# Edge-by-row matrices of a four-layer graph network: made once and loaded by every layer, with the steps of one tile spread over more rounds

## The chip, the cores and the metric

The kernel runs on one core of a Trainium2 chip. Its engines are PE (matrix products), DVE (vector), ACT (scalar, activation functions), POOL (GpSimd) and SP, which here only starts DMAs. Each engine runs its own instructions in order; an instruction waits for what it needs through semaphores. The metric is the device time of one execution in microseconds, the median of several runs.

## The reference

Four graph layers over 4096 nodes of 256 features each work on the same adjacency matrix `adj` (4096 x 4096, about nine neighbours a node beside the node itself). Each layer normalizes the rows of x, takes the positive part, computes attention scores for every pair of nodes, masks them with `adj`, takes a softmax over the neighbours, and adds the weighted sum to x:

```
for layer in (0, 1, 2, 3):
    h = maximum(layernorm(x), 0)
    x = x + gnn[layer](h, adj, ...)
```

Layer 0 has eight heads, with a bias from curvature features. Layer 1 has one head with leaky-ReLU scores from two vectors. Layer 2 takes two softmaxes, of e and of -e, and multiplies both results with a matrix `wtrans`. Layer 3 has four heads whose scores are products of the rows themselves; entries that are not neighbours count there as score 1.

## The kernel before

The kernel does not form the dense attention matrix. `gnn_lists` finds the edges and works on lists: the 4096 rows are 32 tiles of 128, and each tile has up to 9 x 128 = 1152 places for edges (EC = 9 chunks of 128). For each tile there is a matrix of zeros and ones that says which edge belongs to which row. It is needed in two orientations: rows on the partitions, edges along the free axis (`st`, 128 x 1152), and edges on the partitions, rows along the free axis (`s`, nine chunks of 128 x 128).

**Layer 0** runs together with the reading of the adjacency matrix. `piece` (L1094) loads 512 KB of it and turns it into a mask, `pack` (L1112) packs masks into keys by products, `rank` (L1134) sorts out the keys of a tile, `columns` (L1219) and `places` (L1255) decode them for four tiles at a time, `mark` (L1294) makes `st` of a tile and stores it to `rows_of` in DRAM, and `find_edges` (L1303) puts the column number of each edge on the partition of the edge by products with `st`, and writes it to `nbr`. Then come the steps of a tile: `begin0` (L1328) starts the gather of the neighbours' rows, `before0` (L1335) brings the row's own scores to its edges (L1343) and transposes the nine chunks of `st` on PE (L1355), which ACT copies into `s_f` (L1356); `score0`, `turn_d`, `curve` and `weigh0` compute the weights and multiply the gathered rows with them (L1388); `attend0` (L1390) sums over the edges by products with `s_f` (L891); `finish0`, `turn1` and `rows1` normalize the new rows and store the table of layer 1. All these are put on a plan with a due time each (from L1421 on), and are issued in the order of these times: PE works in exactly this order, and the order on the other engines is settled when the program is built.

**Gathers.** `gather` (L879) starts nine indirect DMAs on POOL (L881) for a tile, one a chunk, each of 128 rows of the table, and one DMA on SP (L885) for the tile's own rows. A layer's gathers need the whole table that the layer before has written. G0 = 5 and G1 = 6 are the numbers of buffers for gathered rows.

**Layers 1 to 3** are each a call of `run` (L1493), which issues rounds. In round r each step works on tile r minus the step's lag, so a step of lag 1 works on the tile before the one of lag 0. `loads` (lag -3) loads `st` and x of a tile through SP; `begin` (lag 2 - G1 = -4) starts the gather. `before12` (L1516) brings the row's scores to the edges and calls `s_chunks` (L1486), nine transposes into a PSUM tile `s_ps`. `weigh1` (L1540) and `weigh2` (L1607) compute the weights w and multiply `s_ps` with them into `sw` on DVE (L1545, L1620). `attend1` and `attend2` sum over the edges by products with `sw` (L891, L1636). `finish1`, `turn2`, `rows2`, and in layer 2 `signed2`, `turn_signed`, `through_wt`, `finish2`, `turn3`, `rows3`, complete the tile and store the table of the next layer. In layer 3 `before3` (L1719) casts `st` and the transposed chunks to float on ACT, and `weigh3`, `attend3`, `finish3` follow. The lags of layers 1 and 2 are in these lines (L1584 and L1704):

```
(0, weigh1), (1, finish1), (0, attend1), (1, turn2), (-1, before12(own[0])), (1, rows2),
(0, weigh2), (1, signed2), (2, finish2), (0, attend2), (2, turn3), (1, turn_signed),
(2, rows3), (-1, before12(own[1])), (1, through_wt),
```

In layers 0 and 3 the product of the gathered rows with the weights takes the weights from PSUM: ACT writes them there first (L1385, L1751).

## Time and profile before

| | us |
|---|---|
| median of 14 runs | 1741.99 |
| lowest and highest of them | 1736.57, 1747.43 |
| the profiled execution | 1739.59 |
| its span | 1737.9 |

Busy time over the span: PE 1339.5 us, DVE 1050.6, ACT 584.2, POOL 1113.8. The first gather starts at 132.5 us. The gathers of layer 0 are started from then to 533 us, those of layer 1 from 569 to 929, of layer 2 from 951 to 1313, of layer 3 from 1344 to 1705; the span ends 33 us later. HBM is read at 289.60 MB and written at 43.29 MB.

In the lines of a profile, L881 is line 881 of the kernel; `out<-in` names the tiles; `x32` is the number of instructions; "busy, mean ns" is followed by the idle time of the engine just before them and what ended it. "SPq" and "ACTq" are DMA starts on these engines' queues. PE's clock is given as the share of full speed that it was granted.

### The profile page before, as it was taken

The page shows a single profiled execution, that of the slowest core. Times are in us where ns is not written, and L with a number is a line of the kernel's source. Part 1 is how long each engine was busy: PE and PEld are TensorE (multiplying, and loading weights), DVE is VectorE, ACT ScalarE, POOL GpSimd, SP SyncE. Part 2 cuts the span into 40 slices and gives each one's busy share as a digit, 9 for nine tenths or more (in the row PEclk, how much of TensorE's full clock was granted, in tenths as well). Part 3 has the DMA queues.
Part 4 walks back from the last instruction along what each step waited for, and adds up shares of the span by engine and source line. Part 5 has one row for each costly group of instructions (what it writes and reads, how often), then busy time and mean ns, then how long its engine had stood idle before and what let it go on. Part 6 is the DMA issues. An engine that isn't in the chain of part 4 may idle for free.

```text
span 1737.9 us, 26840 instructions
## 1 busy us (share of the span) xinstructions
PE 1339.5 (77%) x8560; PEld 1072.3 (62%) x8560; DVE 1050.6 (60%) x3038; ACT 584.2 (34%) x1586; POOL 1113.8 (64%) x1208
## 2 busy tenths in 40 slices
PE   3765888878897477666675689988897798898984
PEld 2443666656776365555564577777775577776773
DVE  4675898888874233333332355555554688888884
ACT  2675666763432011111111133333343222222220
POOL 2007775755771677777773777777772777777771
PEclk9996898988998678878887799999998899999998
DMA  8988999984662666767664566666653555555541
GB/s 278 304 274 301 307 351 340 332 299 125 189 174 70 192 172 180 182 182 178 179 171 129 147 169 178 182 179 181 171 173 92 151 170 156 169 169 165 168 134 45
DMA packets 178342, 334.81 MB, mean 193 GB/s; under 512 B 36624, under 2 KB 108560, under 8 KB 178192
## 3 DMA queue, kind: packets, MB, share of 16 engines
q0 software_dynamic: 55296, 153.72, 33.3%
q1 hardware_dynamic: 73730, 133.50, 23.5%
q10 hardware_dynamic: 49166, 45.79, 7.7%
q8 instruction: 70, 1.15, 0.3%
q14 instruction: 80, 0.66, 0.1%
HBM read 289.60 MB, written 43.29 MB: 192 GB/s over the span
## 4 chain that ended last, share of the span: by engine, by line
PE 34%; POOL 16%; DVE 16%; DMA 13%; issue 10%; ACT 3%; DVEq 0%; ACTq 0%; POOLq 0%; SPq 0%
PE o L891 21%; POOL g L881 16%; DMA g<-table,nbr 11%; PE o L1636 3%; PE pt L851 2%; DVE sw L1545 2%; PE pv L1737 2%; DVE s L1742 2%; DVE sw L1620 2%; DVE v L1741 1%; DVE r L824 1%; PE kps L1120 1%; DVE stats L821 1%; PE pb L1343 1%; PE pt L842 1%
## 5 line engine op out<-in xcount | busy, mean ns | idle before, releaser
L881 POOL DMA_INDIRECT g<-table,nbr x1152 | 1097.9, 953 | 484.6 <-issue 311.1
L891 PE MATMUL o<-g,sw 128*128 128x257 f32 x640 | 214.0, 509 | 117.9 <-DVE sw L1548 117.9
L891 PE MATMUL o<-g,s_f 128*128 128x264 f32 (+1 forms) x1152 | 283.7, 403 | 0.0
L891 PEld LDWEIGHTS o<-g,sw 128*128 128x128 f32 x640 | 165.6, 264 | 156.4 <-DVE sw L1548 121.0
L891 PEld LDWEIGHTS o<-g,s_f 128*128 128x128 f32 x1152 | 234.2, 203 | 44.4
L1636 PE MATMUL o<-g,sw 128*128 128x257 f32 x768 | 185.5, 400 | 59.2 <-DVE sw L1620 59.2
L1636 PEld LDWEIGHTS o<-g,sw 128*128 128x128 f32 x768 | 150.2, 199 | 94.0 <-DVE sw L1620 71.3
L1737 PE MATMUL pv<-g,st_f 128*128 128x256 f32 x576 | 146.1, 400 | 45.9 <-DVE v L1741 45.9
L844 ACT COPY hT<-pt 128x256 f32<-128x256 f32 x128 | 47.3, 369 | 329.0 <-PE pt L842 321.3
L1737 PEld LDWEIGHTS pv<-g,st_f 128*128 128x128 f32 x576 | 107.7, 196 | 72.4 <-DVE v L1741 59.6
L1559 DVE RECIPROCAL inv<-o 128x1 f32<-128x1 f32 x32 | 5.4, 168 | 217.0 <-PE o L891 217.0
L1101 ACT ACTIVATE mask<-adj,minus_half 128x1024 bf16<-128x1024 int32 x112 | 124.8, 1142 | 31.1 <-DVE same L929 15.4
L1741 DVE TENSOR_TENSOR v<-pv,g 128x512 f32<-128x512 f32 (+1 forms) x160 | 96.1, 633 | 47.8 <-DMA g<-table,nbr 41.5
L851 PE MATMUL pt<-wcat,hT 128*128 128x272 f32 (+2 forms) x384 | 92.1, 357 | 25.2 <-ACT hT L844 25.1
L851 PEld LDWEIGHTS pt<-wcat,hT 128*128 128x128 f32 x384 | 64.8, 196 | 47.9 <-ACT hT L844 40.4
L1754 DVE TENSOR_TENSOR g<-g,pm 128x2560 f32<-128x2560 f32 x32 | 90.1, 2817 | 3.9 <-ACT pm L1751 3.8
L1388 DVE TENSOR_TENSOR g<-g,pb 128x2560 f32<-128x2560 f32 x32 | 90.1, 2815 | 1.2 <-ACT pb L1385 1.2
L1120 PE MATMUL kps<-mask,enc 128*128 128x512 bf16 x256 | 80.8, 416 | 3.9 <-ACT mask L1101 3.5
L1742 DVE TENSOR_REDUCE s<-v 128x36 f32<-128x2304 f32 x32 | 81.5, 2547 | 0.1
L1722 ACT CAST st_f<-st 128x1152 f32<-128x1152 bf16 x32 | 36.8, 1152 | 111.3 <-PE pv L1737 110.6
L842 PE MATMUL pt<-ident,r 128*128 128x128 f32 x256 | 52.0, 286 | 27.3 <-DVE r L824 20.7
L1176 POOL COPY row<-cv 128x6 f32<-128x6 f32 x32 | 6.9, 218 | 102.3 <-DMA table<-row 54.5
(279 smaller groups left out, 2147.2 us busy)
## 6 DMA issues: line engine op xcount, KB each, us to landing
adj<-in_adj_l SPq DMA_DIRECT2D x128, 512.0 KB
st<-rows_of SPq DMA_DIRECT2D x96, 288.0 KB
g<-table,nbr POOLq DMA_INDIRECT x1152
x<-x ACTq DMA_DIRECT2D x96, 128.0 KB
x<-x SPq DMA_DIRECT2D x96, 128.0 KB
rows_of<-st ACTq DMA_DIRECT2D x32, 288.0 KB
table<-row ACTq DMA_DIRECT2D x64, 129.0 KB
g<-table SPq DMA_DIRECT2D x64, 129.0 KB
```

The source lines that it names most:

```text
L842: nc.tensor.transpose(pt[:, k, :], h[:, k * P : (k + 1) * P], ident)
L851: nc.tensor.matmul(pp, lhsT=hT[:, k, :], rhs=w[:, k, :], start=(k == 0), stop=(k == KC - 1))
L881: nc.gpsimd.indirect_dma_start(out=g[:, c, :width], out_offset=None, in_=table[:, :], in_offset=bass.IndirectOffsetOnAxis(ap=nbr[:, t, c : ...
L891: nc.tensor.matmul(o, lhsT=a, rhs=b, start=(i == 0), stop=(i == len(pairs) - 1))
L1101: nc.scalar.activation(m, a, AF.Sign, bias=minus_half, scale=1.0)
L1120: nc.tensor.matmul(kps[h][:KP, :RG], lhsT=enc[0 if on_dve(r, k) else 1][:, at, :], rhs=m[:, i, :], start=False, stop=(at == HB - 1),)
L1388: nc.vector.tensor_mul(gh, gh, w[:, :, :, None].to_broadcast([P, K, H0, D0]))
L1636: nc.tensor.matmul(o, lhsT=sw[:, h, i].rearrange("p s r -> p (s r)"), rhs=g[:, c, : C + 1], start=(i == 0), stop=(i == 5),)
L1737: nc.tensor.matmul(pv[:, k, :], lhsT=st[:, (a + k) * P : (a + k + 1) * P], rhs=g[:, SELF, :C], start=True, stop=True,)
L1741: nc.vector.tensor_mul(v[:, a : a + n, :], pv[:, :n, :], g[:, a : a + n, :C])
L1742: nc.vector.tensor_reduce(s[:, :EC, :], heads(v, K3), AX.X, OP.add)
L1754: nc.vector.tensor_mul(gh, gh, w[:, :, :, None].to_broadcast([P, K, K3, D3]))
```

## The change

- `find_edges` brings, beside the column of an edge, the number of its row to the edge's partition: the lists `both` and `edge` get one more column, made from `row_no`, and ACT copies the result to `row_of`.
- `before0` makes the edge-by-row matrix from it with one comparison on DVE: `s_b` is one where the edge's row equals `row_nos`. `s_b` (bf16) is stored to the second half of `rows_of`, which is now 128 x 2 x 1152, and cast to `s_f` for layer 0. The transposes and their copies from PSUM go.
- `loads` fetches both matrices, 576 KB a tile, into ST = 5 buffers in place of 288 KB into 4. `s_chunks` and its PSUM tile go; `chunks` names the second half of the loaded tile. `weigh1`, `weigh2` and `before3` read it from SBUF.
- G1 becomes 7. `attend1` and `attend2` and the steps behind them come one round later, `before12` one round earlier, and in layer 2 `turn_signed` and `through_wt` are issued ahead of `turn3` and `rows3`. Some PSUM pools get more banks.

```
-G0, G1 = 5, 6
+G0, G1 = 5, 7
+ST = 5
-    rows_of = [dram.tile([P, EC * P], BF16, name=f"rows_of{t}") for t in range(NT)]
+    rows_of = [dram.tile([P, 2, EC * P], BF16, name=f"rows_of{t}") for t in range(NT)]
...
+            nc.vector.memset(row_no, 0.0)
+            nc.vector.tensor_scalar(row_no[:, 0:1], number, 1.0, None, op0=OP.add)
+            nc.vector.tensor_scalar(row_nos, place_i, 0.5, 1.0, op0=OP.mult, op1=OP.add)
...
-            both = find.tile([P, GT, 2, K], FP16, name="both")[:, :n]
+            both = find.tile([P, GT, 2, K + 1], FP16, name="both")[:, :n]
+            nc.vector.tensor_copy(both[:, :, :, K], row_no[:, None, :].to_broadcast([P, n, 2]))
...
-            store(rows_of[t], st)
+            store(rows_of[t][:, 0, :], st)
...
+            of0[t]["row"] = find.tile([P, EC], F32, name="row_of", bufs=6)
+            nc.scalar.copy(of0[t]["row"], pe[:, :, K])
...
+            s_b = work.tile([P, EC, P], BF16, name="s_b")
+            nc.vector.tensor_tensor(
+                s_b, row_nos[:, None, :].to_broadcast([P, EC, P]),
+                of0[t].pop("row")[:, :, None].to_broadcast([P, EC, P]), op=OP.is_equal,
+            )
+            store(rows_of[t][:, 1, :], s_b.rearrange("p c r -> p (c r)"))
             s = of0[t]["s"] = work.tile([P, EC, P], F32, name="s_f")
-            for a, b in ((0, 8), (8, EC)):
-                pt = bank(ps_t, "pt", BF16)[:, : (b - a) * P].rearrange("p (c r) -> p c r", r=P)
-                for c in range(a, b):
-                    nc.tensor.transpose(pt[:, c - a, :], st[:, c * P : (c + 1) * P], ident_b)
-                nc.scalar.copy(s[:, a:b, :], pt)
+            nc.scalar.copy(s, s_b)
...
-        def s_chunks(st):
-            pt = ps_s.tile([P, EC + 7, P], BF16, name="s_ps")[:, :EC, :]
-            for c in range(EC):
-                nc.tensor.transpose(pt[:, c, :], st[:, c * P : (c + 1) * P], ident_b)
-            return pt
+        def chunks(st):
+            return st[:, 1, :].rearrange("p (c r) -> p c r", c=EC)
...
-                of[t]["st"] = fetch(work, rows_of[t], [P, EC * P], "st", BF16, bufs=4)
-                of[t]["x"] = fetch(work, tile_rows(x_of, t), [P, C], "x", bufs=6)
+                of[t]["st"] = fetch(work, rows_of[t], [P, 2, EC * P], "st", BF16, bufs=ST)
+                of[t]["x"] = fetch(work, tile_rows(x_of, t), [P, C], "x", bufs=7)
...
-            steps = [(-3, loads), (2 - G1, begin)] + [
+            steps = [(2 - ST, loads), (2 - G1, begin)] + [
...
                 nc.vector.tensor_mul(
-                    sw[:, :EC, :], of.pop("s"), w[:, :EC, None].to_broadcast([P, EC, P])
+                    sw[:, :EC, :], chunks(of.pop("st")), w[:, :EC, None].to_broadcast([P, EC, P])
                 )
...
-                    (0, weigh1), (1, finish1), (0, attend1), (1, turn2), (-1, before12(own[0])),
-                    (1, rows2),
+                    (0, weigh1), (2, finish1), (1, attend1), (2, turn2), (-2, before12(own[0])),
+                    (2, rows2),
...
-                        halves(of.pop("s"), P, HP, [[0, 2], [1, HP]]),
+                        halves(chunks(of.pop("st")), P, HP, [[0, 2], [1, HP]]),
...
-                    (0, weigh2), (1, signed2), (2, finish2), (0, attend2), (2, turn3), (1, turn_signed),
-                    (2, rows3), (-1, before12(own[1])), (1, through_wt),
+                    (0, weigh2), (2, signed2), (3, finish2), (1, attend2), (2, turn_signed), (3, turn3),
+                    (-2, before12(own[1])), (2, through_wt), (3, rows3),
...
-                nc.scalar.copy(st_f, st)
+                nc.scalar.copy(st_f, st[:, 0, :])
                 s = of["s"] = work.tile([P, EC, P], F32, name="s_f")
-                nc.scalar.copy(s, s_chunks(st))
+                nc.scalar.copy(s, chunks(st))
```

## The prediction

> **What bounds the kernel now.** I read the page first, then busy times by stage, then the waits of POOL, then the timeline around single gathers. The page's costliest group is the gather of neighbour rows, nine per tile on POOL:
>
> ```profile
> L881 POOL DMA_INDIRECT g<-table,nbr x1152 | 1097.9, 953 | 484.6 <-issue 311.1
> ```
>
> One gather is busy for 0.95 us and is followed by 0.30 us put down to "issue", so POOL cannot start one more often than every 1.25 us: 288 gathers of a layer take 360 us. Busy time by stage (window, length, PE, PEld, DVE, ACT, POOL, clock, DMA share, GB/s) for layers 1, 2 and 3:
>
> ```profile
> 568.00:930.00 362.00, 246.65 (x1345) 206.09 (x1346) 124.63 (x407) 48.03 (x180) 272.80 (x288) 0.78 0.68 179
> 951.00:1313.00 362.00, 305.58 (x1810) 251.68 (x1811) 178.63 (x539) 125.52 (x556) 274.57 (x288) 0.95 0.61 173
> 1344.00:1706.00 362.00, 311.55 (x1521) 257.64 (x1519) 296.11 (x401) 91.71 (x188) 273.66 (x288) 0.95 0.54 159
> ```
>
> Three layers with very different PE and DVE loads take the same time, and each holds all its 288 gathers: POOL sets their pace. Its waits (total, times, longest):
>
> ```profile
> POOL g L881 <- issue: 311.1, 999, 2.9
> ...
> POOL g L881 <- DMA x<-x: 36.3, 2, 36.0
> POOL g L881 <- PE pm L1710: 30.8, 1, 30.8
> POOL g L881 <- PE o L891: 27.1, 47, 8.3
> POOL g L881 <- DMA table<-row: 22.2, 2, 21.9
> ```
>
> 36.0, 21.9 and 30.8 are the gaps before layers 1, 2 and 3, where the next table must be complete. The waits on PE o lie in layer 0 (280 to 455 us), where buffers of g come free late: there PE and DVE set the pace, 14 us a tile, and from 458 to 514 us PE alone, 9.3 us a tile. So the span of 1737.9 us is: 132.5 to the first gather; 436 for layer 0 with its gap; 382 and 393 for layers 1 and 2 with theirs; 361 for layer 3; 33 of drain. The profiled execution took 1739.6 us, 2.4 under the median of 1742.0.
>
> **What the views of totals hide.** Some gathers last longer than 0.95 us. In the timeline they are those that start while a DVE instruction with both operands in SBUF runs:
>
> ```profile
> 1206.25 0.42 DVE L1680 SCALAR_TENSOR_TENSOR x<-low,x 128x256 f32<-128x256 f32 x1
> 1206.30 1.19 POOL L881 DMA_INDIRECT g<-table,nbr  x1 [0.30 <-DVE low L1679]
> ```
>
> A far longer DVE instruction with one operand in PSUM (s_ps) does nothing to a gather that starts inside it:
>
> ```profile
> 922.86 1.35 DVE L1545 TENSOR_TENSOR sw<-s_ps,w 128x1152 f32<-128x1152 bf16 x1
> ...
> 922.98 0.95 POOL L881 DMA_INDIRECT g<-table,nbr  x1 [0.30 <-issue]
> ```
>
> I went through all 1152. Of the gathers that start inside L1545 (34), L1754 (71) or L1388 (57), all with a PSUM operand, none is delayed by more than 0.01 us. With L1680, L1769, L1403, L1563, L1623 (both operands in SBUF, 0.42 us) every gather that starts over 0.05 us after the DVE instruction is late by (end of the DVE instruction minus start of the gather minus 0.127 us); the delays reach 0.26 us. The DVE instruction that starts after the gather costs it nothing.
>
> **The change part by part.**
>
> *Layers 1 and 2, the product with w.* The nine transposes into s_ps go; L1545 and L1620 now read the matrices from SBUF (st) and w from SBUF. Their rows now:
>
> ```profile
> L1545 DVE TENSOR_TENSOR sw<-s_ps,w 128x1152 f32<-128x1152 bf16 x32 | 43.2, 1349 | 0.3 <-ACT w L1543 0.3
> L1620 DVE TENSOR_TENSOR sw<-s_ps,w 128x640 f32<-128x640 bf16 x64 | 49.8, 820 | 19.1 <-ACT w L1612 18.5 <-PE pt L1669 0.6
> ```
>
> I keep their durations (the 256-element rows with SBUF operands are no slower than those with PSUM: 0.42 to 0.43 against 0.42 to 0.48). They become instructions with two SBUF operands, and POOL is the pace. A gather that starts at a random moment of its 1.25 us period loses e²/(2·1.25), e being the duration less 0.147 us. For L1680 this gives 0.031 us a tile, 1.0 us in 32; its eight measured delays add to 1.4. L1545: e = 1.20, 0.58 us a tile, 18 us in the layer. L1620: e = 0.67, 0.18 us each, 64 times: 12 us. Bounds: a weighing that always falls between two gather starts costs 0; one that always catches a start early costs 1.2·32 = 38 us in layer 1 and 0.67·32 = 21 in layer 2, or 45 if a gather waits through both halves (where DVE instructions run back to back in layer 0, the gather mostly gets in at the end of the first). The weighing follows the landing of its own gather by about a microsecond, so the phase is not quite random; landings spread over 1 us or more (2.75 to 5.1 us after the last gather's start in layer 3), and I take the random value.
>
> On this the Trainium skill speaks twice. "GPSIMD Engine Reference", section Key points, says POOL shares its SBUF interfaces with VectorE and contends with DVE instructions that have two SBUF inputs, which is against this change. "SBUF — State Buffer", section Who interferes with whom, narrows it to POOL instructions that read SBUF and infers that descriptor generation is not touched by tensor_tensor; by that the sum would have 0 in place of the 30 us. The rows above side with the first page.
>
> *Layers 1 to 3, what goes.* PE loses nine transposes a tile (0.66 us) and PE waits 118 us in layer 1 for sw as it is; nothing of it is on the path, POOL covers it. Layer 3 casts st and s on ACT from SBUF (1.15 us by row L1722, as now); ACT is off the path and has no part in the delays. Layer 3: 0.
>
> *Loads doubled to 576 KB* (96 of them, 28 MB more) on SP. DMA share in the layers is 0.54 to 0.68 at 160 to 180 GB/s, while 345 GB/s are seen at 200 us: 25 GB/s more are hidden. If they were not, landings would come later, which costs time at the four drains alone.
>
> *Steps over more rounds.* The gathers of a tile are issued one round earlier with one more buffer; POOL has nothing else in its queue and never waits for a buffer in these layers, so 0. On SP the load of a tile's own rows passes one tile's st and x, which waits for the store of x of seven tiles before; as POOL and not the order of rounds holds the tiles back, that lies some five rounds (56 us) behind, so 0. Relative to attend the PE order of layer 1 is unchanged except that the small products of before12 come two rounds earlier; weigh no longer stands behind finish on DVE. At the end of layer 1, s of the last tile starts at 934.0, behind that work, 3 us after its gather could land: I take 2 us of the gap. In layer 2 turn_signed and through_wt now stand before turn3 and rows3, so that in the drain the product at 1332.2 need not wait for rows3 (2.07 us): 2 us. Together -4 (0 to -7).
>
> *Layer 0.* Out: nine transposes (0.66 us of PE a tile) and two casts from PSUM (1.01 + 0.27 us of ACT). In: on DVE is_equal over 1152 elements, 1.35 us by row L1545; on ACT a cast of 1152 (1.15), a copy of nine columns (0.19, row L1525) and one more store's issue (0.33), so ACT gains 0.4; 288 KB of DMA; and is_equal too has two SBUF operands. From 132 to 455 us DVE is busy 264 of 323 us and PE 256: 24 tiles bring DVE 32 us more, so 92%, and take 16 us from PE. The chain there is over half PE and a quarter DVE; with a quarter to a half of the 32 on the path (8 to 16) and half of the 16 gone, +4 (-4 to +14). From 455 on DVE has room (55 of 78 us) and the casts stand on the chain: 0.4 us off 9.3 for ten tiles, -4 (-1 to -6; below that the last landing at 536 holds). Gathers here lose 0.58 us a tile too, covered by POOL's waits for buffers, 27 us and more. Adjacency loads share DMA at 0.94, but ACT waits for them only this long:
>
> ```profile
>   DMA adj<-in_adj_l: 14.5, 7
> ```
>
> and in the packet records each piece lands 1.3 to 14 us ahead of its mask from the fortieth on, so 0.9 us more DMA a tile is covered. Setup: 0.6 us of small DVE instructions, off the path. Layer 0: 0 (-6 to +14).
>
> Sum: 18 + 12 - 4 + 0 = +26. 1739.6 becomes 1765.6 for the profiled execution, 1742 becomes 1768 for the median.
>
> **The rivals.** (1) *The gathers are not held*: the fixed delay from landing to weighing falls between starts, or this form doesn't hold the port. Then only -4 and layer 0 remain: 1738, faster. For: L1620's halves leave a hole. Against: L1545 lasts longer than a whole gather period. It decides where the loss is under 0.06 us a tile over both layers. Chance 0.11. (2) *Layer 0 is set by DVE*: all of the 32 us lands on the path, or the 18 stores in 150 to 380 us (5.3 MB at 330 GB/s, 16 us) push the adjacency back; +20 on the sum, 1788. For: DVE 0.85 and DMA 0.94 busy. Against: the masks' slack, PE relieved. Chance 0.13. (3) The likeliest as summed: 0.76, own range 1752 to 1786.
>
> **How the numbers follow.** The range reaches down towards rival 1 and up through rival 2: 1746 to 1794. Slower by over 0.2% (3.5 us, about what a measurement of this kernel can tell from none): rivals 2 and 3 but for their low ends, 0.86; within 0.2%: 0.04; faster: 0.10.
>
> **What would show it.** In layer 1 the 288 gathers take 375 to 385 us from first to last, in layer 2 370 to 380, in layer 3 still 361; the mean of a gather rises from 953 to about 990 ns, and gathers of 1.1 to 2.1 us begin inside L1545's and L1620's successors. The gaps before layers 2 and 3 shrink to about 20 and 29 us. PE's period after 458 us falls below 9.3. The prediction is wrong if layers 1 and 2 keep their 360 us, or if layer 0 ends more than 14 us later.

## The result

The changed kernel takes 1839.78 us (median of 10 runs, 1828.61 to 1845.38), the kernel before 1742.1 (47 runs). The ratio is 1.0555, 95% interval 1.0537 to 1.0572: 98 us slower. The forecast was slower, 1768 us, with a range up to 1794; the sign was right and the size was not. The profiled execution of the changed kernel took 1848.6 us, with a span of 1846.9, 109 more than the profiled execution before, and some 9 more than its own median; a stage in the table is therefore good to a few us. The first gather, for one, comes at 134.5 to 136.9 us in the profiles of the first six experiments below, so some 3 of its 6.7 are this profile's own.

All stages can be read from the gathers: a stage ends with the last gather of its layer, and a gap is what lies until the next layer's first.

| stage, us | before | after | change | forecast |
|---|---|---|---|---|
| until the first gather | 132.5 | 139.3 | +6.7 | 0 |
| gathers of layer 0, first to last | 400.2 | 430.7 | +30.5 | 0 (-6 to +14), with the gap |
| gap before layer 1 | 36.0 | 46.2 | +10.1 | |
| gathers of layer 1 | 360.2 | 381.8 | +21.6 | +18 |
| gap before layer 2 | 21.9 | 27.5 | +5.6 | -2 |
| gathers of layer 2 | 362.5 | 375.6 | +13.1 | +12 |
| gap before layer 3 | 30.8 | 50.0 | +19.2 | -2 |
| gathers of layer 3 | 361.1 | 360.8 | -0.3 | 0 |
| drain | 32.6 | 35.0 | +2.4 | 0 |
| sum | 1737.9 | 1846.9 | +109 | +26 |

So the loss of the gathers in layers 1 and 2 came as forecast, and two terms that stood at nothing or below are the miss: layer 0 (+47 until the first gather of layer 1) and the drains (+27).

**The gathers.** The page's costliest group, and then the same group in the windows of layers 1, 2 and 3, one line each (instructions, then busy, mean ns of one, then the idle time before them and what ended it):

```profile
L883 POOL DMA_INDIRECT g<-table,nbr x1152 | 1148.2, 997 | 534.2 <-issue 314.4
```

```profile
L883 POOL DMA_INDIRECT g<-table,nbr x288 | 294.3, 1022 | 133.6 <-issue 78.9 <-DMA st<-rows_of 46.2 <-PE o L893 4.6
L883 POOL DMA_INDIRECT g<-table,nbr x288 | 288.1, 1000 | 115.0 <-issue 77.1 <-DMA table<-row 27.5 <-PE o L1648 1.8
L883 POOL DMA_INDIRECT g<-table,nbr x288 | 273.3, 949 | 137.5 <-issue 78.0 <-PE pv L1749 50.3 <-PE o L893 3.7
```

The means of 1022 and 1000 ns are new; layer 3, whose weights stay in PSUM, keeps 949. The products have their old durations:

```profile
L1632 DVE TENSOR_TENSOR sw<-st,w 128x640 f32<-128x640 bf16 x64 | 49.4, 811 | 1.4 <-ACT w L1624 1.1 <-PE o L1648 0.3
L1557 DVE TENSOR_TENSOR sw<-st,w 128x1152 f32<-128x1152 bf16 x32 | 43.3, 1352 | 1.6 <-ACT w L1555 1.6
```

What has changed is what a gather does that starts inside one (timeline):

```profile
989.46 1.35 DVE L1557 TENSOR_TENSOR sw<-st,w 128x1152 f32<-128x1152 bf16 x1
989.60 2.03 POOL L883 DMA_INDIRECT g<-table,nbr  x1 [0.31 <-issue]
```

The DVE instruction ends at 990.81, 1.21 us after the gather started; less 0.127 that is 1.08, and 0.946 + 1.08 = 2.03. I compared every late gather of layers 1 and 2 with this rule: those held by L1557 (30 of them, 20.1 us together) and by L1632 (30, 13.4 us) follow it to within 0.006 us.

**The busy times by stage** (window, length, PE, PEld, DVE, ACT, POOL, clock, DMA share, GB/s) of layers 1, 2 and 3:

```profile
616.00:998.00 382.00, 234.84 (x1056) 189.39 (x1056) 121.55 (x394) 45.03 (x172) 294.30 (x288) 0.77 0.66 196
1025.40:1401.10 375.70, 293.52 (x1457) 243.17 (x1458) 155.29 (x515) 110.55 (x523) 288.14 (x288) 0.88 0.64 190
1451.00:1812.00 361.00, 298.44 (x1224) 249.33 (x1223) 291.26 (x398) 90.96 (x184) 273.33 (x288) 0.89 0.59 175
```

PE has less to do in all three, 12 us in layers 1 and 2 each, and no layer is shorter for it.

**The waits of POOL** (total, times, longest):

```profile
POOL g L883 <- PE pv L1749: 50.3, 2, 50.0
POOL g L883 <- DMA st<-rows_of: 46.5, 2, 46.2
POOL g L883 <- DMA table<-row: 27.5, 1, 27.5
POOL g L883 <- PE o L893: 13.9, 31, 4.8
```

The three longest are the gaps before layers 3, 1 and 2.

**Layer 0 in its second half.** The timeline from the end of one sum over the edges to the start of the next (rows of no weight for the reading are left out):

```profile
517.59 0.21 DVE L1413 RECIPROCAL inv<-o 128x8 f32<-128x8 f32 x1 [2.53 <-PE o L893]
...
518.29 0.42 DVE L1419 TENSOR_TENSOR x<-x,y 128x256 f32<-128x256 f32 x1
...
518.77 1.36 DVE L1366 TENSOR_TENSOR s_b<-row_nos,row_of 128x1152 bf16<-128x1152 bf16 x1
...
520.05 0.42 DVE L823 BATCH_NORM_STATS2 stats<-x 128x6 f32<-128x256 f32 x1
...
520.72 0.35 DVE L826 TENSOR_SCALAR r<-x,mv 128x256 f32<-128x256 f32 x1
...
521.22 0.41 PE L844 MATMUL pt<-ident,r 128*128 128x128 f32 x2 [2.03 <-DVE e L1381]
```

The same stretch of the kernel before:

```profile
471.85 0.21 DVE L1397 RECIPROCAL inv<-o 128x8 f32<-128x8 f32 x1 [0.42 <-PE o L891]
...
472.55 0.42 DVE L1403 TENSOR_TENSOR x<-x,y 128x256 f32<-128x256 f32 x1
...
473.01 0.43 DVE L821 BATCH_NORM_STATS2 stats<-x 128x6 f32<-128x256 f32 x1
...
473.30 0.66 PE L1355 MATMUL pt<-ident_b,st 128*128 128x128 bf16 x9
...
474.32 0.41 PE L842 MATMUL pt<-ident,r 128*128 128x128 f32 x2 [0.36 <-DVE e L1365]
```

The comparison L1366 belongs to a later tile and is in no hurry, but in DVE's queue it stands between x + y and the statistics of the tile whose sum has just ended, and PE's next products wait for these. PE waits 2.03 us there, where before it waited 0.36 us behind its nine transposes (L1355). From the end of the sum to the turn it is 3.67 us, where it was 2.5 to 2.65 before. Averages over tiles 21 to 26, in us: the sum takes 6.28 (before 4.72), from its end to the turn 3.73 (2.59), from there to the next sum 1.97 (2.00); the period is 12.0, and was 9.3.

**The clock.** The sum has grown while PE's granted clock has fallen; the third experiment tests whether the one comes from the other. Second half of layer 0, before and after:

```profile
458.00:515.00 57.00, 51.84 (x553) 43.34 (x553) 43.93 (x108) 23.33 (x65) 43.29 (x46) 0.99 0.69 190
```

```profile
490.00:560.00 70.00, 56.99 (x493) 47.24 (x492) 46.72 (x113) 22.93 (x61) 52.38 (x50) 0.79 0.63 182
```

The records give the clock in steps of 3.41 us, each at full or at half speed. Before, the steps from 449.3 to 514.2 us are all at full speed; after, from 498 to 570 us, one or two at half follow every two at full.

**The end of layers 1 and 2.** The timeline around the last landing of layer 1:

```profile
999.86 0.17 DVE L1540 TENSOR_TENSOR s<-g,a 128x10 f32<-128x10 f32 x1 [7.83 <-DMA g<-table,nbr]
...
1000.02 0.48 DVE L1572 SCALAR_TENSOR_TENSOR x<-o,inv,x 128x256 f32<-128x256 f32 x1
```

The first is the score of tile 31, which waited 7.83 us for its gather; right behind it stands finish1 of tile 29, whose sum had ended at 995.6. Tile 29's turn, and on PE the sum of tile 30 behind it, come after that. So two sums are left after the last score:

```profile
1004.17 7.43 PE L893 MATMUL o<-g,sw 128*128 128x257 f32 x20
...
1012.75 4.59 PE L893 MATMUL o<-g,sw 128*128 128x257 f32 x20
```

Before it was one:

```profile
934.02 0.17 DVE L1532 TENSOR_TENSOR s<-g,a 128x10 f32<-128x10 f32 x1
...
936.71 6.29 PE L891 MATMUL o<-g,sw 128*128 128x257 f32 x20 [3.24 <-DVE sw L1548]
```

From the last score to the next layer's first gather it is 25.6 us instead of 16.8. In layer 2 it is 46.1 us instead of 28.8, with two sums and four products with wtrans begun (1410.0, 1421.0, 1430.7, 1436.5), where one sum and two products (1324.4, 1332.2) were left before.

### The profile page after: what moved, and what is told of

Same layout as the page of the kernel before. It is cut to its first block, busy times and chain, and to the rows that moved or that the text cites. A ratio compares the mean times of both kernels' runs of the same rounds, so it can differ in the third digit from the quotient of the medians.

```text
span 1846.9 us, 24559 instructions
## 1 busy us (share of the span) xinstructions
PE 1339.9 (73%) x7408; PEld 1063.4 (58%) x7408; DVE 1066.1 (58%) x3082; ACT 579.7 (31%) x1586; POOL 1165.0 (63%) x1208
## 5 line engine op out<-in xcount | busy, mean ns | idle before, releaser
L883 POOL DMA_INDIRECT g<-table,nbr x1152 | 1148.2, 997 | 534.2 <-issue 314.4
L893 PE MATMUL o<-g,s_f 128*128 128x264 f32 (+1 forms) x1152 | 312.0, 432 | 0.0
L893 PEld LDWEIGHTS o<-g,s_f 128*128 128x128 f32 x1152 | 255.5, 222 | 54.7
L1540 DVE TENSOR_TENSOR s<-g,a 128x10 f32<-128x10 f32 x64 | 11.0, 171 | 439.0 <-DMA g<-table,nbr 422.9
L893 PE MATMUL o<-g,sw 128*128 128x257 f32 x640 | 207.6, 497 | 14.5 <-DVE sw L1560 14.5
L1648 PE MATMUL o<-g,sw 128*128 128x257 f32 x768 | 177.5, 388 | 20.1 <-DVE sw L1632 20.1
L844 PEld LDWEIGHTS pt<-ident,r 128*128 128x128 f32 x256 | 32.8, 158 | 221.7 <-issue 156.7
L853 PE MATMUL pt<-wcat,hT 128*128 128x272 f32 (+2 forms) x384 | 103.2, 387 | 64.8 <-ACT hT L846 64.2
L1749 PE MATMUL pv<-g,st_f 128*128 128x256 f32 x576 | 135.0, 389 | 3.9 <-DVE v L1753 3.9
L1749 PEld LDWEIGHTS pv<-g,st_f 128*128 128x128 f32 x576 | 112.2, 195 | 21.9 <-DVE v L1753 5.8
L893 PE MATMUL o<-g,ident 128*128 128x264 f32 (+1 forms) x128 | 58.6, 550 | 63.2 <-DVE g L1766 63.2
L1681 PE MATMUL pt<-wt_s,two_t 128*128 128x256 f32 x256 | 85.7, 493 | 18.4 <-ACT two_t L1672 17.6
```

What stands on the lines that cost most here:

```text
L844: nc.tensor.transpose(pt[:, k, :], h[:, k * P : (k + 1) * P], ident)
L853: nc.tensor.matmul(pp, lhsT=hT[:, k, :], rhs=w[:, k, :], start=(k == 0), stop=(k == KC - 1))
L883: nc.gpsimd.indirect_dma_start(out=g[:, c, :width], out_offset=None, in_=table[:, :], in_offset=bass.IndirectOffsetOnAxis(ap=nbr[:, t, c : ...
L893: nc.tensor.matmul(o, lhsT=a, rhs=b, start=(i == 0), stop=(i == len(pairs) - 1))
L1648: nc.tensor.matmul(o, lhsT=sw[:, h, i].rearrange("p s r -> p (s r)"), rhs=g[:, c, : C + 1], start=(i == 0), stop=(i == 5),)
L1681: nc.tensor.matmul(pp, lhsT=lhs[:, k, :], rhs=wt_s[:, k, :], start=(k == 0), stop=(k == 2 * KC - 1))
```

## The experiments

My theory after the result (A in the expectations): four separate causes, each with its place: held gathers in layers 1 and 2, longer drains from the later rounds, the comparison's place in layer 0, and the clock that falls with it. The first four runs share one chip and the runs of the kernel before, 1740.43 us there. The changed kernel has no run on that chip; differences from it are taken from its 1839.78 us above.

### The later rounds undone

```
-G0, G1 = 5, 7
+G0, G1 = 5, 6
-                    (0, weigh1), (2, finish1), (1, attend1), (2, turn2), (-2, before12(own[0])),
-                    (2, rows2),
+                    (0, weigh1), (1, finish1), (0, attend1), (1, turn2), (-1, before12(own[0])),
+                    (1, rows2),
...
(layer 2: lags and order of the kernel before)
```

> The changed kernel with the spreading undone: lags, order and G1 = 6 of layers 1 and 2 as before, everything else (both matrices loaded, comparison in layer 0) as changed. Theory A (the later rounds lengthen the drains: more tiles' sums and products are left when the last gather has landed): the gaps before layers 2 and 3, 27.4 and 50.0 us in the changed kernel, go back to 22 +- 3 and 31 +- 3; layer 0 and the 382 and 376 us of gathers in layers 1 and 2 stay; time 1840 - 25 = 1815 (1808 to 1822). Rival B (the drains are long because 576 KB a tile are loaded and land late): the gaps stay at 27 and 50 and the time at 1840.

Measured: 1829.69 us, ratio to before 1.0489 (1.0436 to 1.0542). The gaps of 27.5 and 50.0 became 19.2 and 33.7:

```profile
POOL g L883 <- PE pv L1749: 33.7, 1, 33.7
POOL g L883 <- DMA table<-row: 19.2, 1, 19.2
```

Both are as theory A says, and the loads of 576 KB were still there, so rival B is out: the drains come from the lags, G1 and layer 2's order, which this edit undoes together. The time, however, fell by 10 us and not by 25 (the spans of the profiled executions differ by 17, as that of the changed kernel lies above its median). In this run's profile layer 1's gathers took 388.8 us, 7 more than in the changed kernel: the product fell on worse moments of the gather's period (31 of 31 caught a gather, 26.4 us together, where 30 had lost 20.1). The price of the product thus depends on its phase, and the phase differs from kernel to kernel: in the five profiles with both operands in SBUF (the changed kernel, this run and three of those below) it is 17.0 to 26.4 us over layer 1.

### w of layer 1 in PSUM

```
+        ) as ps_t, tc.tile_pool(name="l1_w", bufs=2, space=PSUM) as ps_w:
...
-                w = work.tile([P, EC + 1], F32, name="w")
-                nc.scalar.activation(w, s, AF.Exp)
+                w = bank(ps_w, "pw")[:, :EC]
+                nc.scalar.activation(w, s[:, :EC], AF.Exp)
+                w_l = work.tile([P, 1], F32, name="w_l")
+                nc.scalar.activation(w_l, s[:, SELF:], AF.Exp)
...
```

> The changed kernel with one edit in layer 1: ACT writes the weights w to PSUM, so that the product with the loaded matrix has one operand in PSUM; layer 2 is left alone. Theory A (a product with two operands in SBUF holds back a gather that starts while it runs): the 288 gathers of layer 1 take 361 us from first to last in place of 382, with a mean of 948 ns in place of 1022; those of layer 2 keep 376 us; time 1840 - 21 = 1819 (1812 to 1825). Rival B (the gathers are slowed by the 28 MB of added loads): layer 1 keeps 382 us, time 1840.

Measured: 1820.88 us, ratio 1.0450 (1.0408 to 1.0492), 19 us less than the changed kernel. Gathers of layer 1, and for comparison of layer 2, which was left alone:

```profile
L883 POOL DMA_INDIRECT g<-table,nbr x288 | 272.6, 947 | 135.0 <-issue 77.7 <-DMA st<-rows_of 47.5 <-PE o L893 3.7
L883 POOL DMA_INDIRECT g<-table,nbr x288 | 286.5, 995 | 113.4 <-issue 75.2 <-DMA table<-row 26.0 <-PE o L1650 2.1
```

Layer 1 is back at 947 ns and at 360.1 us from first to last, with the doubled loads running; layer 2 keeps 995. The product lasts 1.35 us as before, and what differs is where its second operand lies (and one more small activation on ACT). That settles the cause of the 21 us, and that the loads have no part in it.

### PE's gap in layer 0 filled

```
+            dead = bank(ps_t, "pt", BF16).rearrange("p (c r) -> p c r", r=P)
+            for c in range(16):
+                nc.tensor.transpose(dead[:, c % 8, :], st[:, c % 8 * P : (c % 8 + 1) * P], ident_b)
             s_b = work.tile([P, EC, P], BF16, name="s_b")
```

> The changed kernel with sixteen dead transposes put back on PE in before0 of layer 0, where the nine were; nothing reads them. Theory A (in the second half of layer 0 PE waits so long that its granted clock falls to half every other 3.4 us, and the sums over the edges take 6.3 us in place of 4.7): with the gap filled the clock in 490 to 560 us rises above 0.9, the sum takes about 4.7 us, a tile 10.6 to 11 us in place of 12.0, and layer 1 starts 6 to 14 us earlier; time 1826 to 1834. Rival B (the clock has nothing to do with the gap, or the added products stand on the path): no gain, 1838 to 1850.

Measured: 1819.41 us, ratio 1.0436 (1.0387 to 1.0485): 20 us less, by adding work that nothing reads. The second half of layer 0:

```profile
490.00:560.00 70.00, 61.52 (x593) 52.01 (x591) 50.42 (x110) 23.92 (x64) 54.16 (x53) 0.93 0.64 189
```

The clock rose from 0.79 to 0.93. Most sums take 4.72 us again, tiles 21 to 23 have a period of 9.9 us although their sum still ends 3.67 us ahead of the turn, and layer 1 starts at 594.5 us instead of 616.1. So of the 47 us about 20 are the clock, 17 of them behind the start of tile 20's sum (474.1 in the changed kernel, 469.4 here). Both the start of layer 1, 21.6 us earlier by the profiles where I had expected 6 to 14, and the time are better than expected. The period of 9.9 us also splits the 12.0 of the changed kernel: 9.3 before, 1.1 more from the sum's end to the turn, 0.5 less from the turn to the next sum (1.5 instead of 2.0, as the casts to s_f no longer stand there on ACT), and 2.1 for the lower clock. What lets the clock fall, the longer wait or the nine transposes that PE no longer has, these sixteen don't separate; the next run undoes both.

### Layer 0's transposes back, no comparison

```
-            s_b = work.tile([P, EC, P], BF16, name="s_b")
-            nc.vector.tensor_tensor(
...
+            store(rows_of[t][:, 1, :], st)
             s = of0[t]["s"] = work.tile([P, EC, P], F32, name="s_f")
-            nc.scalar.copy(s, s_b)
+            for a, b in ((0, 8), (8, EC)):
...
+                nc.scalar.copy(s[:, a:b, :], pt)
```

> The changed kernel with layer 0's transposes and casts as before and without the comparison; the row numbers are still made and the second store still done, but of st itself, so that layers 1 to 3 work with a wrong matrix of the same size. Theory A (the comparison on DVE is what lengthens layer 0, by its place after the sum over the edges and by its load in the first half): layer 1's first gather, at 569 before and 616 us after the change, comes at 570 to 580; a tile of the second half takes 9.3 us again; time 1840 - 40 = 1800 (1793 to 1808). Rival B (the second store and the wider lists cost layer 0 its time, through DMA and the order in which the work is issued): first gather of layer 1 still after 595, time over 1819.

Measured: 1810.71 us, ratio 1.0397 (1.0354 to 1.0440), 29 us less than the changed kernel; layer 1's first gather comes at 578.5 us. (This kernel leaves out the second matrix: layers 1 to 3 load st in its place, of the same size.) The time is 3 us above the expected range, the place of the gain as expected: layer 0 has a period of 9.3 us in its second half and the clock is full:

```profile
467.00:524.00 57.00, 51.70 (x565) 43.25 (x562) 44.51 (x108) 23.71 (x72) 43.28 (x46) 1.00 0.75 211
```

So the comparison with what follows from it costs layer 0 some 36 us (614, the mean of the first gathers of layer 1 in the changed kernel and the two runs above with an unaltered layer 0, less 578.5). The 10 us that are left against 568.7 lie ahead of tile 20's sum, which starts at 457.9 us here and at 447.7 before. 3 of them are the later first gather (135.5 here); the wider lists and the second store are what else is left of the change there, and they were not taken apart. The 47 us of layer 0 divide at the start of tile 20's sum: 26 ahead of it (474.1 for 447.7) and 21 behind it (142 us to layer 1's first gather for 121, and 120.6 in this run).

### The comparison made twice

```
...
             store(rows_of[t][:, 1, :], s_b.rearrange("p c r -> p (c r)"))
+            twin = work.tile([P, EC, P], BF16, name="twin", bufs=1)
+            nc.vector.tensor_tensor(
+                twin, row_nos[:, None, :].to_broadcast([P, EC, P]),
+                of0[t]["row"][:, :, None].to_broadcast([P, EC, P]), op=OP.is_equal,
+            )
```

> The same kernel as e6_equal_twice, once more, alone, in the hope of a chip without the long stalls. Theory A (the comparison of layer 0 costs by its place in the second half, by DVE's load in the first): the period of 12.0 us after 490 us stays within 0.4 us, the first half grows by 8 to 18 us; time 1848 to 1860. Rival B (load everywhere): period up by 1 us and more, time 1865 to 1880. Rival C (place alone): under 1845.

Measured (kernel before 1745.05 there): 1869.25 us, ratio 1.0702 (1.0655 to 1.0749), in rival B's range; the period over tiles 21 to 26 is 13.1 us, also as rival B says. But the expectation had a wrong premise: one more instruction changes the order of the others. Of tiles 20 to 27 only tile 21 has the second comparison in its chain; in the others it begins 1.6 us or more ahead of the end of PE's sum, or is not there at all. The first one, however, now stands in some tiles ahead of y, and there it waits for a cast on ACT while all that the turn needs stands behind it:

```profile
528.62 0.21 DVE L1418 RECIPROCAL inv<-o 128x8 f32<-128x8 f32 x1 [0.96 <-PE o L893]
...
529.80 1.36 DVE L1366 TENSOR_TENSOR s_b<-row_nos,row_of 128x1152 bf16<-128x1152 bf16 x1 [0.94 <-ACT s_f L1377]
...
531.15 0.42 DVE L1420 TENSOR_TENSOR y<-o,inv 128x256 f32<-128x256 f32 x1
...
533.75 0.66 PE L844 MATMUL pt<-ident,r 128*128 128x128 f32 x2 [3.54 <-DVE r L826]
```

In this tile (22) it is 5.17 us from the sum to the turn, and 14.0 to the next sum. In tile 23 the first comparison stands after x + y, as in the changed kernel, and the second runs under the sum: 3.67 us and 12.1, the changed kernel's figures with 1.35 us more on DVE. So where the second comparison is covered, as in tile 23, the added load costs nothing, and the place of the first makes a difference of 1.5 us from the sum to the turn between tiles 22 and 23. In the first half, where DVE has little to spare, load counts: tile 20's sum starts at 494.3 us instead of 474.1, and as the first gather was 2.7 us earlier that is 22.9 us for some 20 more comparisons of 1.35 (27 us), though changes of order are in this figure too. The first comparison, with the transposes gone, had cost less there: 474.1 in the changed kernel against 457.9 with the transposes, 12.4 us after the difference of the first gathers.

### All mended but the change itself

The edits of the first three experiments together, and w of layer 2 in PSUM as well:

```
-        with tc.tile_pool(name="l2_o", bufs=2, space=PSUM) as ps_o, tc.tile_pool(
+        with tc.tile_pool(name="l2_o", bufs=1, space=PSUM) as ps_o, tc.tile_pool(
...
+        ) as ps_t, tc.tile_pool(name="l2_w", bufs=2, space=PSUM) as ps_w:
...
-                w = work.tile([P, EC + 1, 2], F32, name="w2")
+                w = bank(ps_w, "pw")[:, : 2 * (EC + 1)].rearrange("p (c s) -> p c s", s=2)
```

> The same kernel as e7_mended, alone, right after a run without the long stalls. Theory A (the four causes are separate and add): gathers of layers 1 and 2 take 361 and 362 us, the gaps before layers 2 and 3 are 20 and 32, and what is left against the kernel before is layer 0 alone, 20 to 28 us; time 1760 to 1770. Rival B (a cause that no part shows): a stage other than layer 0 stays over 5 us longer, time over 1775.

Measured (kernel before 1742.75 there): 1784.78 us, ratio 1.0241 (1.0216 to 1.0266). That is 55 us better than the changed kernel, and 42 slower than the kernel before; rival B's case, since one stage did not come back:

```profile
POOL g L883 <- DMA table<-row: 39.7, 1, 39.7
POOL g L883 <- DMA st<-rows_of: 34.1, 1, 34.1
POOL g L883 <- PE pv L1754: 32.6, 1, 32.6
```

Gathers of layers 1 and 2 take 361.8 and 362.3 us, the gap before layer 3 is 32.6, layer 1 starts at 590.5 (before 568.7): as expected. The gap before layer 2 is 39.7 us, not 20. The times from a tile's last gather to its score in layer 1 show why: they grow from 3.6 us at the first tile to 21.4 at the last. With old lags the score of a tile stands on DVE behind finish1 of the tile before, and that behind its sum, so that sum (6.83 us on average), normalizing, score, product and the next sum are one chain. Its period is 11.92 us against the 11.25 of nine gathers on POOL. In the kernel before the same chain takes 11.38, and the distance grows from 2.0 to 5.1 us only; with the later rounds and w in PSUM (the second experiment) it stays at 1.9 to 4.5 us, 2.5 at the last tile. So the later rounds do buy something: they break a chain that is almost hidden in the kernel before. With the gathers held, as in the first experiment, it is hidden too, and only the lengthening of the drain shows.

Why the chain is half a microsecond longer than before can be read from the order on DVE. Before, x + bias of the tile before stands ahead of the score:

```profile
932.88 0.42 DVE L1563 TENSOR_TENSOR x<-x,bias 128x256 f32<-128x256 f32 x1
...
934.02 0.17 DVE L1532 TENSOR_TENSOR s<-g,a 128x10 f32<-128x10 f32 x1
...
935.05 1.35 DVE L1545 TENSOR_TENSOR sw<-s_ps,w 128x1152 f32<-128x1152 bf16 x1
```

In this run it stands between the score and the product:

```profile
962.43 0.17 DVE L1543 TENSOR_TENSOR s<-g,a 128x10 f32<-128x10 f32 x1 [0.19 <-DVE own L1593]
962.52 0.42 DVE L1580 TENSOR_TENSOR x<-x,bias 128x256 f32<-128x256 f32 x1
...
963.92 1.35 DVE L1562 TENSOR_TENSOR sw<-st,pw 128x1152 f32<-128x1152 bf16 x1
```

It does so in 31 of 32 tiles here and in 1 of 32 before; from score to product it is 1.49 us on average instead of 1.06, and the sum takes 6.83 us instead of 6.69. It is again an instruction's place, which no run moved back.

Undoing causes one at a time (10, 19 and 20 us, and 13 for layer 2 by its profile) makes 62 us; together they gave 55. The chain just described shows that they are not independent. None of these versions beats the kernel before, and no stage shows a gain from the transposes that the change takes off PE. The one gain seen on the path is that of the casts on ACT, 0.5 us a tile in the second half of layer 0.

### Runs in which engines stall

The experiments "made twice" and "all mended" were first run three and four times, on the chips numbered 1, 9, 14 and 10, while engines stalled there. The two runs above, without the stalls, came later, on the chips numbered 10 and 1: the chip alone does not decide it. What was expected of "all mended" there:

> Everything mended at once that can be without giving up the change: the changed kernel with the old lags and order of layers 1 and 2 (G1 = 6), w in PSUM for the products of layers 1 and 2, and sixteen dead transposes in before0 of layer 0. Theory A (the four causes are separate and add): gathers of layers 1 and 2 take 361 and 362 us, the gaps before layers 2 and 3 are 20 and 32, and what is left against the kernel before is layer 0 alone, 20 to 28 us; time 1760 to 1770. Rival B (a cause that no part shows, such as the added loads, is left): a stage other than layer 0 stays over 5 us longer, time over 1775.

> The same kernel as e7_mended again, since the chip of that run had slow transfers and its stages say nothing of the four causes. Theory A (the causes add): gathers of layers 1 and 2 take 361 and 362 us, the gaps before layers 2 and 3 are 20 and 32, and only layer 0 is left, 20 to 28 us; time 1760 to 1770. Rival B (a cause that no part shows): a stage other than layer 0 stays over 5 us longer, time over 1775.

> The same kernel as e7_mended, for a chip without the long stalls. Theory A (the four causes are separate and add): gathers of layers 1 and 2 take 361 and 362 us, the gaps before layers 2 and 3 are 20 and 32, and what is left against the kernel before is layer 0 alone, 20 to 28 us; time 1760 to 1770. Rival B (a cause that no part shows): a stage other than layer 0 stays over 5 us longer, time over 1775.

> The same kernel as e7_mended, once more, alone, in the hope of a chip without the long stalls. Theory A (the four causes are separate and add): gathers of layers 1 and 2 take 361 and 362 us, the gaps before layers 2 and 3 are 20 and 32, and what is left against the kernel before is layer 0 alone, 20 to 28 us; time 1760 to 1770. Rival B (a cause that no part shows): a stage other than layer 0 stays over 5 us longer, time over 1775.

And of the comparison made twice:

> The changed kernel with the comparison of layer 0 made twice, the second into a tile that nothing reads; by the order that the kernel is built with, the second stands after the weighing, while PE sums, and not between the sum and the normalizing. Theory A (in the second half of layer 0 the comparison costs by its place, in the first half about half of its time by DVE's load): the period of 12.0 us after 490 us stays within 0.4 us, the first half grows by 8 to 18 us; time 1848 to 1860. Rival B (it costs by DVE's load everywhere): the period of the second half grows by 1 us and more, time 1865 to 1880. Rival C (by its place alone): under 1845.

> The same kernel as e6_equal_twice again (the comparison of layer 0 made twice, the second while PE sums). Theory A (place in the second half, DVE's load in the first): the period of 12.0 us after 490 us stays within 0.4 us, the first half grows by 8 to 18 us; time 1848 to 1860. Rival B (load everywhere): period up by 1 us and more, time 1865 to 1880. Rival C (place alone): under 1845.

> The same kernel as e6_equal_twice (the comparison of layer 0 made twice, the second while PE sums), for a chip without the long stalls. Theory A (place in the second half, DVE's load in the first): the period of 12.0 us after 490 us stays within 0.4 us, the first half grows by 8 to 18 us; time 1848 to 1860. Rival B (load everywhere): period up by 1 us and more, time 1865 to 1880. Rival C (place alone): under 1845.

The transfers of the change alone, three times:

```
(kernel before, transfers alone)
...
+            store(rows_of[t][:, 1, :], st)
-                of[t]["st"] = fetch(work, rows_of[t], [P, EC * P], "st", BF16, bufs=4)
+                of[t]["st"] = fetch(work, rows_of[t], [P, 2, EC * P], "st", BF16, bufs=4)[:, 0, :]
```

> The kernel before with the transfers of the change alone: every st is stored twice (two halves of rows_of), and layers 1 to 3 load both halves, 576 KB a tile; the transposes stay and the second half is not read by any engine. Theory A (the added 28 MB of loads are hidden and the added store costs layer 0 little): layers 1 to 3 keep 360 to 363 us of gathers and their gaps; layer 0 takes 0 to 8 us more; time 1740 to 1749. Rival B (the transfers cost what layer 0 still lacks with its transposes back, and more in the drains): over 1752.

> The same kernel as e3_loads again (the kernel before with the added transfers alone). Theory A (hidden): layers 1 to 3 keep 360 to 363 us of gathers and their gaps; layer 0 takes 0 to 8 us more; time 1740 to 1749. Rival B (the transfers cost what layer 0 still lacks with its transposes back): over 1752.

> The same kernel as e3_loads (the kernel before with the added store and loads alone), for a chip without the long stalls. Theory A (the transfers are hidden): layers 1 to 3 keep 360 to 363 us of gathers and their gaps; layer 0 takes 0 to 8 us more; time 1740 to 1749. Rival B (the transfers cost what layer 0 still lacks with its transposes back): over 1752.

The order of layer 2 alone:

```
(kernel before, order of layer 2 alone)
-                    (0, weigh2), (1, signed2), (2, finish2), (0, attend2), (2, turn3), (1, turn_signed),
-                    (2, rows3), (-1, before12(own[1])), (1, through_wt),
+                    (0, weigh2), (1, signed2), (2, finish2), (0, attend2), (1, turn_signed), (2, turn3),
+                    (-1, before12(own[1])), (1, through_wt), (2, rows3),
```

> The kernel before with one part of the change, the order of layer 2: turn_signed and through_wt are issued ahead of turn3 and rows3, all lags as before. Theory A (my prediction's step: in the drain the product need not wait for rows3): the gap before layer 3 falls from 30.8 to 28 to 30 us, time 1738 to 1741, which the medians alone can't tell from 1742. Rival B (the order is put back when the kernel is built, or the product waits for something else): the gap stays at 30.8, or grows.

The changed kernel, unaltered:

> The changed kernel once more, unaltered, on the chip of these runs, as the yardstick of the parts. On a chip on which the kernel before takes about 1742: 1835 to 1845. On the chip of the last four runs, where transfers are slow: faster than the kernel before, since e6, which only adds work to it, was faster there (0.94); theory: with gathers that land late the seventh buffer and the later rounds pay.

In these runs the kernel before took 2453 to 2498 us. Engines stood still for tens of us without an event that the profile can name. Some waits of the changed kernel there:

```profile
DVE v L1753 <- remote: 191.0, 33, 46.1
...
PEld pt L844 <- issue: 136.8, 40, 33.7
...
ACT hT L846 <- remote: 124.3, 14, 30.8
```

Ratios to the kernel before, same chip and time: the changed kernel 0.933 (0.926 to 0.940), the comparison made twice 0.942, 0.942 and 0.955, all mended 0.962, 0.968, 0.981 and 0.976, the transfers alone 0.989, 0.996 and 0.997, the order of layer 2 alone 0.951 (0.942 to 0.960). So there the changed kernel is the faster by 6.7%; that it would be faster was expected. Its deeper run-ahead is a possible reason, its smaller number of products on PE (7408 against 8560) another; nothing here tells them apart. The expectations in times, made for a kernel before of 1742 us, can't be judged here; the transfers alone have no run without stalls. What these runs do show, as it does not hang on the stalls: with w in PSUM the mean gather of layers 1 and 2 was 946 to 956 ns in all four mended runs, and 989 to 1024 in the four with both operands in SBUF; and with the transfers alone it was 945 to 953, as in the profile before (947 and 955). Whether the new order of layer 2 shortens the drain, as I had said, is not settled: the gap there was 71.6 us, with the stalls in it.

## Why the prediction was right or wrong

The forecast of slower was right, and two of its steps failed: the comparison in layer 0, which was priced by DVE's load alone, and the later rounds, which were to shorten the drains. The prediction's own sign of being wrong came: layer 0's gathers end at 570.0 us instead of 532.7, more than 14 later.

1. *POOL sets the pace of layers 1 to 3, and a product with two operands in SBUF holds a gather.* Right, in mechanism and in size: 20.1 us for layer 1 (forecast 18), 13.4 for layer 2 (12), and the second experiment takes the loss of layer 1 away by moving one operand. "GPSIMD Engine Reference", section Key points, of the Trainium skill states the contention with DVE instructions that have two SBUF inputs, and these runs agree; the narrower inference in "SBUF — State Buffer", section Who interferes with whom, would have given 0 and is contradicted by them. That the random phase came within 2 us is partly luck: the same product lost 17.0 to 26.4 us in the other kernels.

2. *"From 455 on DVE has room (55 of 78 us) and the casts stand on the chain: 0.4 us off 9.3 for ten tiles, -4."* Here the mechanism failed. Room in a sum over a window says nothing of an instruction's place in an in-order queue. The comparison stands between a tile's sum and its normalizing, 1.14 us longer from the sum's end to the turn. PE now pauses 2.0 us in each tile, with nine transposes fewer, and its clock falls to half for a part of the time, 1.56 us more a sum; the clock was no term of the forecast. The 0.4 for the casts did come (0.5 in the third experiment) but was covered by this. Measured: period 12.0 instead of 9.3, in place of 8.9, and 21 us more from tile 20's sum on in place of 4 less. The clock's share, about 17 us, is shown by the third experiment; that the comparison and what follows from it are the rest, by the fourth.

3. *"With a quarter to a half of the 32 on the path (8 to 16) and half of the 16 gone, +4 (-4 to +14)", for the first half.* Measured: 26 us until tile 20's sum. 12.4 are the comparison with the transposes gone, where 0 to 8 were forecast (8 to 16 less 8); whether the comparison's share was larger or PE's relief smaller is not separated. Some 10 us, in which the wider lists and the second store lie, stay with the transposes back and were priced at nothing. The other 4 are the difference between the first gathers of the two profiles.

4. *"Steps over more rounds" at 0 for POOL and SP, and the drains at "-4 (0 to -7)".* Wrong in sign: +27 in the profile, of which the first experiment takes 24.6 away in the two gaps. I had weighed the rounds in the steady state, where POOL covers them, and looked in the drain only for what comes earlier. A lag raised by one leaves one tile more unfinished when the last gather lands, and with in-order queues the finish of an older tile waits behind the score that waits for that landing. Whether the new order of layer 2 alone gives the 2 us claimed for it is open.

5. *Loads doubled: 0.* Right: 360.1 us for layer 1 in the second experiment and 360.8 for layer 3 after the change, both with 576 KB a tile.

6. The rival "layer 0 is set by DVE, +20", chance 0.13, had the right stage and direction. Its price was too low because it, too, counted load and no place, and no rival had the clock or the drains.

## What to carry to other kernels

An instruction moved to an engine with room is free only if its place in that engine's order is: read which instructions it will stand between, and who waits for the later one. Work taken off PE, or a pause added there, can cost time by the clock (here dead work brought 20 us back); look at the granted clock by stage before counting relief as gain. The rounds of lag added here were paid at each of the two drains, so count the tiles that are unfinished when the last input lands; and when a gather on POOL sets the pace, let one operand of long DVE products lie in PSUM.

## What the runs showed of the hardware

**The clock has a threshold between busy and idle.** Over the steps of 3.41 us of the two profiles, every step at full speed in which PE was busy for less than 0.40 was followed by one at half (48 of 48 before, 56 of 56 after), and of those busy for more than 0.65 all but one were followed by full (286 of 287 and 234 of 234). Between 0.40 and 0.65 both came. A step at half speed that was busy for less than 0.8 was followed by half in all cases (36 and 66), and one busy for over 0.95 mostly by full (59 of 61, 82 of 89). In the second half of layer 0 after the change the longest pause of PE is 2.4 us. "TensorE: Matmul & The Clock Gate" of the Trainium skill, section What's actually happening, gives half speed after at least one idle window of about 3.4 us; the length of the window agrees, but none of the steps at full speed that were followed by half there (490 to 560 us) was idle: 0.40 to 0.57 busy was enough, and the measurement decides.

**A held gather is held by the rule** end of the DVE instruction less start of the gather less 0.127 us, for durations of 0.42 to 1.35 us, and no longer: 33 gathers of layers 1 and 2 after the change, inside which one of the two products starts later, are late by 0.035 us at most.

**Dead work on PE can pay:** sixteen transposes a tile that nothing reads, with a clock of 0.93 instead of 0.79 in the second half of layer 0, 20 us of 1840.
